# Two stages changed at once: 7x7 filter rows loaded to half of the partitions and copied across by VectorE, and a last pass whose first layer runs in three parts of two slices instead of two parts of three

## The chip, the cores and the metric

One NeuronCore of a Trainium2 chip runs the whole program. The metric is device time in microseconds (us): the median of several executions. All arithmetic is float32. The engines are named as in the profile: PE is TensorE (matmuls), PEld is its weight load, DVE is VectorE, ACT is ScalarE, POOL is GpSimd, SP is SyncE, which here only issues transfers. Transfers can be issued from SP, ACT or POOL.

## The reference, cut to what matters

The input `x` is 8 images of 96 x 96 pixels with 192 channels. Two residual blocks follow one another. The first has a projection to 384 channels, a 3x3 depthwise convolution, four directional scans, a layer norm and a projection back. The second, which is the one that the change touches, is

```python
def _L1_conv_ref(x, dw_kernel, dw_bias, ln_gamma, ln_beta, w0, b0, w1, b1, gamma):
    y = lax.conv_general_dilated(x, dw_kernel, window_strides=(1, 1), padding='SAME',
            dimension_numbers=('NHWC', 'HWIO', 'NHWC'), feature_group_count=c) + dw_bias   # 7x7 depthwise
    mu = jnp.mean(y, axis=-1, keepdims=True)
    var = jnp.mean(jnp.square(y - mu), axis=-1, keepdims=True)
    y = (y - mu) * lax.rsqrt(var + EPS) * ln_gamma + ln_beta
    y = jnp.einsum('bhwc,cd->bhwd', y, w0) + b0        # first layer: 192 -> 768
    y = jax.nn.gelu(y, approximate=False)
    y = jnp.einsum('bhwd,dc->bhwc', y, w1) + b1        # second layer: 768 -> 192
    return y * gamma

x = x + _L0_conv_ref(_gn(x), ...)
x = x + _L1_conv_ref(_gn(x), ...)                      # _gn: group norm with 32 groups of 6 channels
```

## The kernel before

The program has five stages, one after another. A projects to 384 channels, B convolves 3x3 and scans, C normalizes and projects back, D makes the 7x7 convolution, E is the last pass: layer norm, first layer, Gelu, second layer. Only D and E are touched.

**Stage D.** The convolution is a product with banded matrices. There are 32 steps `m` of `HC` = 6 channels each. A step needs the image rows `xin` and the filter's band `band`, both as tiles of 128 partitions. Partitions 0 to 63 and 64 to 127 hold two different blocks of image rows, and the band is the same in both halves, so it is loaded twice from DRAM:

```python
    def load_d(m):
        c = m * HC
        ...
        pool = d_pools[m % ND > 0]                       # ND = 5 tiles of each kind in all
        xin = pool.tile([128, NT, BP, HC, 2 * WV], F32, tag="xin", name="xin")
        for t in range(NT):                              # NT = 3
            for g, eng in enumerate((nc.sync, nc.gpsimd)):
                ...
                eng.dma_start(xin[g * 64 : (g + 1) * 64, t].rearrange(...), src)
        band = pool.tile([128, HC, ZW], F32, tag="band", name="band1")   # ZW = 208
        for g, eng in enumerate((nc.sync, nc.gpsimd)):
            eng.dma_start(
                band[g * 64 : (g + 1) * 64].rearrange("q c l -> q (c l)"),
                Z2_d[:, c : c + HC].rearrange("r c l -> r (c l)"),
            )
        return band, xin
```

`scale_d` applies the group norm to a loaded `xin` in eight VectorE instructions; the convolution of a pair of steps follows, and its result is stored to DRAM from POOL:

```python
        def scale_d(m, xin):
            xv = xin.rearrange("q t a c (v b) -> q t a c v b", b=2)
            for b in range(B):                           # B = 8
                ...
                nc.vector.tensor_scalar(xw, xw, sc, sh, ALU.mult, ALU.add)

            loads = [first_d] + [load_d(m) for m in range(1, 3)]
            ...
            for i in range(n_i):                         # n_i = 16 pairs
                pair, loads = loads[:2], loads[2:]
                for m in (2 * i + 3, 2 * i + 4):
                    if m < 2 * n_i:
                        loads.append(load_d(m))
                if i + 1 < n_i:
                    for k in range(2):
                        scale_d(2 * i + 2 + k, loads[k][1])
                yo = op.tile([128, NB, BP * NV, HC, 2 * WQ], F32, tag="yo", name=f"yo_{i}")
                for c in range(HC):
                    conv_d(pair, c, yo, i)               # 432 PE instructions for each pair
                store_d(yo, i)
```

The convolution's matmul is line L1021, the store's issues are L1060 (SP) and L1061 (POOL), the loads' issues are L748 (`xin`) and L753 (`band`), the scaling is L1006.

**Stage E.** There are `n_u` = 96 units of 4 x 96 x 2 pixels. Each unit is transposed (`turn_in`, three calls), taken through the first layer into `g` with Gelu on ACT, and through the second layer (`second_layer`, three calls). The 192 input channels of the first layer are 128 + 64: the 128 go as a full matmul, the 64 as a matmul on half of the array's rows, where those of the two images (`q`) lie in different halves:

```python
        ps_t = ph.enter_context(tc.tile_pool(name="e_ps_t", bufs=1, space=PSUM))
        ps_h = ph.enter_context(tc.tile_pool(name="e_ps_h", bufs=7, space=PSUM))
        ...
        def first_layer(u, mb):
            ...
            ms = range(mb * NE // 2, (mb + 1) * NE // 2)     # NE = 6: three slices of 128 of the 768
            for m in ms:
                for q in range(2):
                    hps[m, q] = ps_h.tile([128, WH * S], F32, tag="hp", name="hp")
                    nc.tensor.matmul(hps[m, q], w0w[:, 2 * q, ...], yT[:, 2 * q], start=True, stop=False)   # L1183
            for m in ms:
                for q in range(2):
                    p = slice(q * DH, (q + 1) * DH)          # DH = 64
                    nc.tensor.matmul(hps[m, q], w0w[p, 1, ...], yT[p, 1], start=False, stop=True)           # L1193
            for m in ms:
                for q in range(2):
                    nc.scalar.activation(g[:, m, q], hps[m, q], AF.Gelu, ...)                               # L1202

        def second_layer(u, k):
            ...
            po = ps_h.tile([128, 2, D], F32, tag="hp", name="po")
            for q in range(2):
                for m in range(NE):
                    nc.tensor.matmul(po[:, q], g[:, m, q, k * 128 : (k + 1) * 128], w1g[:, m], ...)         # L1213
            nc.vector.tensor_tensor(xo[:, k]..., po..., rs_[u][:, k], ALU.add)
            ...
```

The order of the calls for a unit (conditions on the first and last units cut):

```python
            for u in range(n_u + 1):
                first_layer(u, 0)
                turn_in(u + 1, 0); load_r(u + 1)
                bias_r(u)
                stats_e(u + 2, j)              # j = 0..3
                second_layer(u - 1, 0)
                turn_in(u + 1, 1)
                first_layer(u, 1)
                turn_in(u + 1, 2)
                stats_e(u + 2, j)              # j = 4..7
                second_layer(u - 1, 1)
                norm_e(u + 2, j)               # j = 0..7
                second_layer(u - 1, 2)
```

Of the kernel before, what the change touches and what calls it, by code (L numbers as in the profile page):

```python
# [8 lines left out]
F32 = mybir.dt.float32  # L9
# [3 lines left out]
PSUM = bass.MemoryType.PSUM  # L13
# [71 lines left out]
def conv_blocks_kernel(  # L85
# [31 lines left out]
    nc = tc.nc  # L117
# [617 lines left out]
    def load_d(m):  # L735
        c = m * HC
        row = D * WV * 2
        pool = d_pools[m % ND > 0]
        xin = pool.tile([128, NT, BP, HC, 2 * WV], F32, tag="xin", name="xin")

        for t in range(NT):
            for g, eng in enumerate((nc.sync, nc.gpsimd)):
                src = bass.AP(
                    tensor=X1_d.tensor,
                    offset=X1_d.offset + (2 * t + g) * HG * PH * row + c * WV * 2,
                    ap=[[row, 64], [S * PH * row, BP], [1, HC * WV * 2]],
                )
                eng.dma_start(  # L748
                    xin[g * 64 : (g + 1) * 64, t].rearrange("q a c n -> q a (c n)"), src
                )  # L750
        band = pool.tile([128, HC, ZW], F32, tag="band", name="band1")
        for g, eng in enumerate((nc.sync, nc.gpsimd)):
            eng.dma_start(  # L753
                band[g * 64 : (g + 1) * 64].rearrange("q c l -> q (c l)"),
                Z2_d[:, c : c + HC].rearrange("r c l -> r (c l)"),
            )
        return band, xin

    s1 = s1_pool.enter_context(tc.tile_pool(name="s1", bufs=1)).tile(
# [228 lines left out]
    with ExitStack() as ph:  # L988
        cp = ph.enter_context(tc.tile_pool(name="d_const", bufs=1))
        d_pools[1] = ph.enter_context(tc.tile_pool(name="d_in", bufs=ND - 1))  # L990
        op = ph.enter_context(tc.tile_pool(name="d_out", bufs=2))
        ps_y = ph.enter_context(tc.tile_pool(name="d_ps", bufs=4, space=PSUM))

        dwb = cp.tile([128, D // CD, HC], F32, name="dwb")
        for k in range(2):
            nc.scalar.dma_start(
                dwb[k * 64 : (k + 1) * 64],
                dw_bias.rearrange("(i k c) -> k i c", k=2, c=HC)[k].partition_broadcast(64),
            )

        def scale_d(m, xin):
            xv = xin.rearrange("q t a c (v b) -> q t a c v b", b=2)
            for b in range(B):
                sc, sh = (s1[:, a, b % 2, b // 2, m : m + 1] for a in range(2))
                xw = xv[:, :, b // 2, :, :, b % 2]
                nc.vector.tensor_scalar(xw, xw, sc, sh, ALU.mult, ALU.add)  # L1006

        def conv_d(pair, c, yo, i):

            pys = [  # L1010
                [ps_y.tile([128, 2, BP, 2 * WV], F32, tag=f"py{a}", name=f"py{a}")
                 for _ in range(2)]
                for a in range(2)
            ]
            for t in range(NT):
                for n, d in enumerate((1, 0, 2)):
                    lo, hi = 2 * max(0, 1 - d), 2 * (WV - max(0, d - 1))
                    for k in range(2):
                        for g in range(2):
                            rows = slice(g * 64, g * 64 + KB)  # L1020
                            nc.tensor.matmul(  # L1021
                                pys[t // 2][g][k * 64 : (k + 1) * 64, t % 2, :, lo:hi],
                                pair[k][0][rows, c, d * ZS : d * ZS + 64],
                                pair[k][1][rows, t, :, c, lo + 2 * (d - 1) : hi + 2 * (d - 1)],
                                start=(n == 0),
                                stop=(n == 2),
                            )
                if t == 0:
                    continue
                for g in range(2):  # L1030
                    bl = slice(g, 4 + g, 2) if t == 1 else slice(4 + g, 5 + g)
                    nc.scalar.activation(
                        yo[:, bl, :, c],
                        pys[t // 2][g][:, : 2 - t // 2].rearrange("q t b (a v) -> q t (b a) v", a=NV),
                        AF.Identity,
                        bias=dwb[:, i, c : c + 1],
                        scale=1.0,
                    )

        def store_d(yo, i):  # L1040
            for bl in range(NB):

                pieces = [(3, HB - 3)]
                if bl == 0:
                    pieces.append((HB - 3, HB))
                if bl == NB - 1:
                    pieces.append((0, 3))
                for k in range(2):
                    c = i * CD + k * HC
                    for lo, hi in pieces:  # L1050
                        r = (S - HB - bl * HG) * PH
                        src = yo[k * 64 + lo * PH : k * 64 + hi * PH, bl]
                        dst = Y_d[r + lo * PH : r + hi * PH, :, :, c : c + HC].rearrange(
                            "r b a c n -> r (b a) (c n)"
                        )
                        src = src.rearrange("r a c n -> r a (c n)")

                        n = NV if i == D // CD - 1 else 0
                        if n:
                            nc.sync.dma_start(dst[:, :n], src[:, :n])  # L1060
                        nc.gpsimd.dma_start(dst[:, n:], src[:, n:])  # L1061

        n_i = D // CD
        with tc.manual_schedule():
            loads = [first_d] + [load_d(m) for m in range(1, 3)]
            make_weights(ps_y.tile([128, 512], F32, tag="py1", name="ps_b0"))
            for m in range(2):
                scale_d(m, loads[m][1])
            for i in range(n_i):
                pair, loads = loads[:2], loads[2:]  # L1070
                for m in (2 * i + 3, 2 * i + 4):
                    if m < 2 * n_i:
                        loads.append(load_d(m))
                if i + 1 < n_i:
                    for k in range(2):
                        scale_d(2 * i + 2 + k, loads[k][1])
                yo = op.tile([128, NB, BP * NV, HC, 2 * WQ], F32, tag="yo", name=f"yo_{i}")
                for c in range(HC):
                    conv_d(pair, c, yo, i)
                store_d(yo, i)  # L1080
    s1_pool.close()

# [8 lines left out]
    with ExitStack() as ph:  # L1094
        ip = ph.enter_context(tc.tile_pool(name="e_in", bufs=2))
        sp = ph.enter_context(tc.tile_pool(name="e_small", bufs=3))
        tp = ph.enter_context(tc.tile_pool(name="e_t", bufs=2))
        ps_t = ph.enter_context(tc.tile_pool(name="e_ps_t", bufs=1, space=PSUM))
        ps_h = ph.enter_context(tc.tile_pool(name="e_ps_h", bufs=7, space=PSUM))

        def place(n):
            bp, n = divmod(n, PH * NV)
# [25 lines left out]
        def bias_r(u):  # L1128
            r = rs_[u].rearrange("p k (b c) -> p (k b) c", b=2)
            nc.gpsimd.tensor_tensor(  # L1130
                r, r, b1g.unsqueeze(1).to_broadcast([128, 2 * S // HE, D]), ALU.add
            )
# [41 lines left out]
        def first_layer(u, mb):  # L1174
            if mb == 0:
                gs[u] = tp.tile([128, NE, 2, WH * S], F32, tag="g", name="g")
            yT, g = yTs[u].rearrange("p k h j -> p k (h j)"), gs[u]
            ms = range(mb * NE // 2, (mb + 1) * NE // 2)
            hps = {}
            for m in ms:  # L1180
                for q in range(2):
# [24 lines left out]
        def second_layer(u, k):  # L1206
            if k == 0:
                xos[u] = tp.tile([128, S // HE, 2, D], F32, tag="xo", name="xo")
            g, xo = gs[u], xos[u]
            po = ps_h.tile([128, 2, D], F32, tag="hp", name="po")  # L1210
            for q in range(2):
                for m in range(NE):
                    nc.tensor.matmul(  # L1213
# [22 lines left out]
        with tc.manual_schedule():  # L1236
# [8 lines left out]
                    for k in range(3):  # L1245
                        turn_in(0, k)
            for u in range(n_u + 1):

                if u < n_u:
                    first_layer(u, 0)  # L1250
                if u + 1 < n_u:
                    turn_in(u + 1, 0)
                    load_r(u + 1)
                if u < n_u:
                    bias_r(u)
                if u + 2 < n_u:
                    for j in range(4):
                        stats_e(u + 2, j)
                if u >= 1:
                    second_layer(u - 1, 0)  # L1260
                if u + 1 < n_u:
                    turn_in(u + 1, 1)
                if u < n_u:
                    first_layer(u, 1)
                if u + 1 < n_u:
                    turn_in(u + 1, 2)
                if u + 2 < n_u:
                    for j in range(4, WE):
                        stats_e(u + 2, j)
                if u >= 1:  # L1270
                    second_layer(u - 1, 1)
                if u + 2 < n_u:
                    for j in range(WE):
                        norm_e(u + 2, j)
                if u >= 1:
                    second_layer(u - 1, 2)


# [45 lines left out]
```

## Time and profile before

The time before is 6060.05 us, the median of three executions from 6058.6 to 6065.66 us. The profiled execution has a span of 6063.8 us.

| stretch of the span | what runs | PE busy | granted PE clock | DMA share | GB/s |
|---|---|---|---|---|---|
| 2900 to 3012 us | end of C | 101.98 of 112 us | 0.98 | 0.78 | 233 |
| 3012 to 3062 us | C to D | 9.52 of 50 us | 0.50 | 0.90 | 238 |
| 3062 to 3540 us | D | 366.98 of 478 us | 0.86 | 1.05 | 284 |
| 3540 to 3631 us | D to E | 44.62 of 91 us | 0.74 | 0.74 | 182 |
| 3631 to 3700 us | E fills | 62.01 of 69 us | 0.92 | 0.25 | 66 |
| 3700 to 6040 us | E | 2340.00 of 2340 us | 1.00 | 0.25 | 69 |

The table comes from the view that gives each engine's busy time by stretch. "DMA share" is the mean busy share of the core's 16 DMA engines; it sums the times of packets, so that overlapping packets can bring it slightly over 1. Over the whole span PE is busy for 5662.7 us (93%), DVE for 3455.4 us (57%), POOL for 2650.1 us (44%) and ACT for 2427.9 us (40%). A matmul of this float32 program shows as two PE instructions, so twelve calls in the code are 24 in the profile. The durations of single matmuls overlap in the record; the distance from one start to the next is what a matmul costs.

### The profile page before, as it was taken

The page shows a single profiled execution, that of the slowest core. Times are in us where ns is not written, and L with a number is a line of the kernel's source. Part 1 is how long each engine was busy: PE and PEld are TensorE (multiplying, and loading weights), DVE is VectorE, ACT ScalarE, POOL GpSimd, SP SyncE. Part 2 cuts the span into 40 slices and gives each one's busy share as a digit, 9 for nine tenths or more (in the row PEclk, how much of TensorE's full clock was granted, in tenths as well). Part 3 has the DMA queues.
Part 4 walks back from the last instruction along what each step waited for, and adds up shares of the span by engine and source line. Part 5 has one row for each costly group of instructions (what it writes and reads, how often), then busy time and mean ns, then how long its engine had stood idle before and what let it go on. Part 6 is the DMA issues. An engine that isn't in the chain of part 4 may idle for free.

```text
span 6063.8 us, 122727 instructions
## 1 busy us (share of the span) xinstructions
PE 5662.7 (93%) x48550; PEld 3970.7 (65%) x48550; DVE 3455.4 (57%) x8026; ACT 2427.9 (40%) x6146; POOL 2650.1 (44%) x2832
## 2 busy tenths in 40 slices
PE   4799989999998999999867759999999999999999
PEld 2455543333334989898756647777777777777777
DVE  5455539999996667777723225444444444444443
ACT  1344437777775555555433322222222222222221
POOL 0111118888886666666534433333333333333332
PEclk9999989999999999999988879999999999999999
DMA  8977759999997888888799982222222222222221
GB/s 235 230 242 226 231 175 243 243 243 244 245 246 203 248 263 264 263 267 262 233 275 284 291 211 60 74 70 72 74 68 76 67 79 63 79 63 79 63 63 38
DMA packets 570206, 1054.36 MB, mean 174 GB/s; under 512 B 109575, under 2 KB 426260, under 8 KB 567328
## 3 DMA queue, kind: packets, MB, share of 16 engines
q1 hardware_dynamic: 385312, 577.65, 36.1%
q0 software_dynamic: 124160, 450.67, 24.1%
q10 hardware_dynamic: 60160, 18.20, 1.5%
q8 instruction: 384, 6.29, 0.5%
q14 instruction: 190, 1.56, 0.1%
HBM read 585.19 MB, written 476.57 MB: 175 GB/s over the span
## 4 chain that ended last, share of the span: by engine, by line
PE 76%; DMA 6%; DVE 1%; issue 1%; SPq 1%; POOL 1%; ACT 0%; DVEq 0%; POOLq 0%; ACTq 0%
PE po L1213 19%; PE po L830 13%; PE hp L1183 12%; PE pl L576 10%; PE hp L1193 7%; PE pa L597 4%; PE pt L828 4%; DMA xin<-X_d 4%; PE py L1021 3%; PE pa L600 2%; PE pt L1166 2%; DMA Y_d<-yo 1%; DVE xin L1006 1%; DMA band<-Z_d 0%; SPq L1060 0%
## 5 line engine op out<-in xcount | busy, mean ns | idle before, releaser
L1202 ACT ACTIVATE g<-hp,b0g 128x384 f32<-128x384 f32 x1152 | 563.5, 587 | 1831.5 <-PE hp L1193 1831.4
L1213 PE MATMUL po<-w1g,g 128*128 128x192 f32 x6912 | 1160.0, 327 | 0.0
L1213 PEld LDWEIGHTS po<-w1g,g 128*128 128x128 f32 x6912 | 1118.8, 190 | 1.1 <-issue 1.1
L830 PE MATMUL po<-wc,mt 128*96 128x193 f32 x4608 | 913.1, 334 | 0.0
L1170 DVE COPY yT<-pt 128x384 f32<-128x384 f32 x288 | 250.0, 868 | 1044.7 <-PE pt L1166 1044.4
L1183 PE MATMUL hp<-yT,w0w 128*128 128x384 f32 x2304 | 781.4, 489 | 0.4 <-DVE yT L1170 0.4
L830 PEld LDWEIGHTS po<-wc,mt 128*96 128x96 f32 x4608 | 702.0, 163 | 68.4 <-ACT mean L834 65.0
L1231 POOL DMA_DIRECT2D out_dram<-xo x576 | 340.2, 593 | 880.9 <-DVE xo L1220 853.7
L576 PE MATMUL pl<-pin,band 34*32 34x380 f32 (+1 forms) x13824 | 628.2, 489 | 18.5 <-DMA pin<-P_d 18.5
L1183 PEld LDWEIGHTS hp<-yT,w0w 128*128 128x128 f32 x2304 | 429.4, 191 | 257.3 <-issue 3.3
L1021 PE MATMUL py<-xin,band 63*64 63x248 f32 (+1 forms) x6912 | 409.0, 396 | 140.7 <-DVE xin L1006 134.9
L606 DVE TENSOR_TENSOR_SCAN z<-decay,loc 128x768 f32<-128x768 f32 x288 | 505.9, 1756 | 58.5 <-ACT loc L585 28.5
L646 POOL TENSOR_TENSOR mo<-mo,z 128x768 f32<-128x768 f32 x288 | 528.9, 1837 | 3.3 <-ACT mo L601 0.2
L29 POOL TENSOR_TENSOR rs<-rs_ve,neg_half 96x8 f32<-96x8 f32 x96 | 158.6, 1652 | 826.3 <-DVE rs_ve L28 826.3
L615 DVE TENSOR_TENSOR_SCAN z<-decay,z 128x768 f32<-128x768 f32 x288 | 498.2, 1730 | 0.0
L576 PEld LDWEIGHTS pl<-pin,band 34*32 34x32 f32 x13824 | 232.0, 107 | 396.6 <-issue 394.5
L1021 PEld LDWEIGHTS py<-xin,band 63*64 63x64 f32 x6912 | 344.4, 143 | 204.9 <-DVE xin L1006 121.2
L837 ACT ACTIVATE sq<-pt,mean 96x384 f32<-96x384 f32 x768 | 442.9, 577 | 25.9 <-ACT mean L834 1.0
L597 PE MATMUL pa<-loc,mix 128*32 128x384 f32 x3456 | 431.7, 493 | 0.0
L375 PE MATMUL pm<-xT,win 128*128 128x384 f32 x1152 | 408.3, 506 | 21.6 <-ACT xT L368 21.1
L600 PE MATMUL pa<-last,down 96*32 96x384 f32 x1152 | 426.6, 493 | 0.9 <-ACT mo L601 0.9
L1193 PE MATMUL hp<-yT,w0w 64*128 64x384 f32 x2304 | 423.5, 500 | 0.0
(116 smaller groups left out, 7726.4 us busy)
## 6 DMA issues: line engine op xcount, KB each, us to landing
P_d<-po POOLq DMA_DIRECT2D x96, 1152.0 KB, 8.8
pin<-P_d SPq DMA_DIRECT2D x192, 576.0 KB
mt<-M_d SPq DMA_DIRECT2D x576, 192.0 KB
xq<-in_x_dram SPq DMA_DIRECT2D x96, 576.0 KB
xr<-in_x_dram SPq DMA_DIRECT2D x384, 144.0 KB
X_d<-x1u POOLq DMA_DIRECT2D x192, 288.0 KB, 4.2
X_d<-x1c SPq DMA_DIRECT2D x192, 288.0 KB
y<-Y_d SPq DMA_DIRECT2D x24, 2304.0 KB
```

Source lines behind the costliest of these rows:

```text
L576: nc.tensor.matmul(pls[g][at * RB : (at + 1) * RB, :, lo:hi], band[rows, c, kh, :], pin[rows, c, :, NJ - 1 - j, lo + kh - 1 : hi + kh - 1] ...
L597: nc.tensor.matmul(pa[at], mix[:, i, at], loc[:, q], start=True, stop=True)
L600: nc.tensor.matmul(pa[at], down[:, to], last[:, q], start=True, stop=True)
L606: nc.vector.tensor_tensor_scan(zf, decay_f, loc.rearrange("p q n -> p (q n)"), 0.0, ALU.mult, ALU.add)
L615: nc.vector.tensor_tensor_scan(zr, decay_f, zr, 0.0, ALU.mult, ALU.add)
L646: nc.gpsimd.tensor_tensor(m, m, z, ALU.add)
L830: nc.tensor.matmul(po[:S, b], lhs[m], wc[:, m], start=(m == 0), stop=(m == NC - 1))
L1021: nc.tensor.matmul(pys[t // 2][g][k * 64 : (k + 1) * 64, t % 2, :, lo:hi], pair[k][0][rows, c, d * ZS : d * ZS + 64], pair[k][1][rows, t, ...
L1183: nc.tensor.matmul(hps[m, q], w0w[:, 2 * q, m * 128 : (m + 1) * 128], yT[:, 2 * q], start=True, stop=False,)
L1193: nc.tensor.matmul(hps[m, q], w0w[p, 1, m * 128 : (m + 1) * 128], yT[p, 1], start=False, stop=True,)
L1202: nc.scalar.activation(g[:, m, q], hps[m, q], AF.Gelu, bias=b0g[:, m : m + 1], scale=1.0)
L1213: nc.tensor.matmul(po[:, q], g[:, m, q, k * 128 : (k + 1) * 128], w1g[:, m], start=(m == 0), stop=(m == NE - 1),)
```

## The change

The change has two parts that have nothing to do with each other.

In D, step `m` loads the band to one half of the partitions only: for even `m` to the lower half from SP, for odd `m` to the upper half from POOL. VectorE then copies it to the other half, ahead of the eight scaling instructions of the same step. It is meant to take bytes from the DMA engines.

In E, the first layer is cut into three parts of two slices (four PSUM banks for a part) instead of two parts of three (six banks). The eight PSUM banks are given out anew: two for the transposes, four for the first layer, and two of its own for the second layer. Each of the three thirds of a unit is then alike: a part of the first layer, a transpose, a part of the second layer.

```diff
         band = pool.tile([128, HC, ZW], F32, tag="band", name="band1")
-        for g, eng in enumerate((nc.sync, nc.gpsimd)):
-            eng.dma_start(
-                band[g * 64 : (g + 1) * 64].rearrange("q c l -> q (c l)"),
-                Z2_d[:, c : c + HC].rearrange("r c l -> r (c l)"),
-            )
+
+        g = m % 2
+        (nc.sync, nc.gpsimd)[g].dma_start(
+            band[g * 64 : (g + 1) * 64].rearrange("q c l -> q (c l)"),
+            Z2_d[:, c : c + HC].rearrange("r c l -> r (c l)"),
+        )
         return band, xin
...
-        def scale_d(m, xin):
+        def scale_d(m, band, xin):
+            g = m % 2
+            nc.vector.tensor_copy(
+                band[(1 - g) * 64 : (2 - g) * 64], band[g * 64 : (g + 1) * 64]
+            )
             xv = xin.rearrange("q t a c (v b) -> q t a c v b", b=2)
...
-        ps_t = ph.enter_context(tc.tile_pool(name="e_ps_t", bufs=1, space=PSUM))
-        ps_h = ph.enter_context(tc.tile_pool(name="e_ps_h", bufs=7, space=PSUM))
+        ps_t = ph.enter_context(tc.tile_pool(name="e_ps_t", bufs=2, space=PSUM))
+        ps_h = ph.enter_context(tc.tile_pool(name="e_ps_h", bufs=4, space=PSUM))
+        ps_o = ph.enter_context(tc.tile_pool(name="e_ps_o", bufs=2, space=PSUM))
...
-            ms = range(mb * NE // 2, (mb + 1) * NE // 2)
+            ms = (2 * mb, 2 * mb + 1)
...
-            po = ps_h.tile([128, 2, D], F32, tag="hp", name="po")
+            po = ps_o.tile([128, 2, D], F32, tag="po", name="po")
...
             for u in range(n_u + 1):
-                ... (the order of calls shown above)
+                for k in range(3):
+                    if u < n_u:
+                        first_layer(u, k)
+                    if u + 1 < n_u:
+                        turn_in(u + 1, k)
+                    if k == 0:
+                        if u + 1 < n_u:
+                            load_r(u + 1)
+                        if u < n_u:
+                            bias_r(u)
+                    if u + 2 < n_u:
+                        if k < 2:
+                            for j in range(4 * k, 4 * k + 4):
+                                stats_e(u + 2, j)
+                        else:
+                            for j in range(WE):
+                                norm_e(u + 2, j)
+                    if u >= 1:
+                        second_layer(u - 1, k)
```

More of the change, by code (lines that the diff above doesn't have):

```diff
@@ L1067, in conv_blocks_kernel @@
             for m in range(2):
-                scale_d(m, loads[m][1])
+                scale_d(m, *loads[m])
             for i in range(n_i):
@@ L1075, in conv_blocks_kernel @@
                     for k in range(2):
-                        scale_d(2 * i + 2 + k, loads[k][1])
+                        scale_d(2 * i + 2 + k, *loads[k])
                 yo = op.tile([128, NB, BP * NV, HC, 2 * WQ], F32, tag="yo", name=f"yo_{i}")
@@ L1247, in conv_blocks_kernel @@
             for u in range(n_u + 1):
[L1249 to L1276, printed above, removed]
+                for k in range(3):
[17 more added lines that the diff above has]
+                        second_layer(u - 1, k)
 _INS = [
```

## The prediction

> **What bounds the kernel now.** The change touches D and E only, so I read the profile by stage. First, busy time by stretch. D in steps of 20 us (columns: stretch, length, busy us of PE, PEld, DVE, ACT, POOL with counts, PE clock, DMA share, GB/s):
>
> ```profile
> 3200.00:3220.00 20.00, 20.00 (x369) 17.26 (x364) 4.01 (x7) 10.47 (x20) 10.67 (x17) 0.96 1.03 314
> 3220.00:3240.00 20.00, 13.14 (x220) 10.84 (x216) 9.53 (x16) 6.26 (x12) 9.62 (x15) 0.83 1.05 269
> 3240.00:3260.00 20.00, 13.64 (x260) 11.42 (x252) 1.99 (x4) 8.41 (x16) 8.38 (x14) 0.90 1.05 279
> 3260.00:3280.00 20.00, 17.19 (x292) 14.93 (x296) 7.66 (x13) 7.54 (x15) 10.38 (x16) 0.84 1.05 340
> 3280.00:3300.00 20.00, 10.72 (x178) 8.81 (x172) 4.81 (x9) 5.03 (x10) 6.37 (x11) 0.76 1.05 240
> ```
>
> PE pauses, DVE is idle most of the time, and the DMA share never leaves 1.03 to 1.05: the DMA engines have no room anywhere. Next, the waits between 3000 and 3600 us (who waited for what: us in total, times, longest):
>
> ```profile
> DVE xin L1006 <- DMA xin<-X_d: 370.3, 31, 26.3
> ...
> PE py L1021 <- DVE xin L1006: 134.9, 17, 20.6
> ```
>
> DVE waits for loaded rows, PE waits for DVE's scaling: 17 waits, one for each pair. The starts of the convolutions in the trace are 33.3 us apart (3196.66 to 3530.01 us is ten pairs), of which PE works 25 and waits 8. D is bound by transfers.
>
> E is the opposite: PE is busy for 2340.00 of 2340 us at clock 1.00, and DMA is at 0.25. The chain that ended last, in order of time, shows one unit (start, length, instruction, count):
>
> ```profile
> 4000.99 7.83 PE po L1213 x48
> 4008.81 3.87 PE hp L1183 x12
> 4012.68 2.14 PE hp L1193 x12
> 4014.82 0.48 PE pt L1166 x4
> 4015.30 3.93 PE po L1213 x24
> 4019.23 0.33 PE pt L1166 x4
> 4019.56 3.90 PE hp L1183 x12
> 4023.46 2.14 PE hp L1193 x12
> 4025.60 0.48 PE pt L1166 x4
> 4026.08 7.83 PE po L1213 x48
> ```
>
> A unit takes 25.09 us, and nothing but PE is on the chain. So E's time is the number of matmuls and the joints between unlike ones. The same transposes take 0.48 us behind a half-array group (L1193) but 0.33 us behind the second layer (L1213). The weight load shows the joint too (waits from 3700 to 6000 us):
>
> ```profile
> PEld hp L1193 <- issue: 99.7, 183, 0.5
> PEld pt L1166 <- issue: 99.7, 183, 0.5
> ```
>
> Each of 183 changes into and out of a half-array group makes the weight load stand 0.54 us with nothing to wait for; the matmuls behind it lose less, since they run on meanwhile.
>
> **What the Trainium skill says.** "TensorEngine Tiling (Array Packing)", Key Properties: a change of the tiling mode drains TensorE. The trace agrees: full matmuls of the first layer start 322.5 ns apart, but the first half-array one starts 416 ns after the last full one, the second pair 420 ns after the first where later pairs take 322, and the first transpose 413 ns after the last pair. "VectorE: DVE Perf Modes", perf-mode tier table: a float32 copy from SBUF to SBUF runs at two elements a cycle. A contiguous float32 scaling of 768 elements (L718) takes 615 ns here, under the 800 ns that one a cycle of its 0.96 GHz would need, so the trace fits. "DMA: Bandwidth & Descriptors", Issuing engines are not separate DMA queues: transfers of SP and POOL share the same 16 engines. D's share of 1.05 whether one or both queues move agrees. "SBUF — State Buffer", two separate sides: such a copy keeps GpSimd from writing the descriptors of its own transfers; no copy of this kind runs beside POOL's transfers before, so nothing here shows what it costs.
>
> **Part one, D: what it removes.** One band load is 64 partitions x 1248 x 4 B = 319,488 B; 32 of the 64 go, 10.2 MB. In the trace, the packets of the loads that disappear (SP's for odd steps, POOL's for even ones) took 17.9 + 20.2 = 38.1 us when summed and divided by 16 engines. With a share of 1.05 that is 36 us of DMA time, or 2.3 us a pair: the upper end. Not all of it need come back. Counting packets in stretches of 2 us, POOL's queue moves only 200 GB/s while it loads alone (380 ns for a packet of 4608 B), but the two queues together 300 to 400. Each pair has some 23.5 us with both and 9.8 us with POOL alone. If SP keeps its own pace, 11% fewer bytes on SP shorten the first stretch to 21 us, in which POOL moves less. Of POOL's 6.54 MB, now 6.22, about 4.09 then pass in the first stretch and 2.13 MB are left, 10.65 us at 200 GB/s: 31.65 us a pair, a gain of 1.65. That is the lower end: 16 x 1.65 = 26 us. I take the middle, **31 us**.
>
> What it adds: 32 copies of 64 x 1248. From L718's 615 ns for 768 elements, between 0.8 us (adding half a cycle for each further element) and 1.0 us (in proportion). DVE is busy for 28 of 100 us in D and has room for two a pair. The copy also makes the scaling wait for the band, which lands after the rows. So rows to convolution grows by some 2.5 us (319,488 B behind the rows at 200 GB/s are 1.6, the copy 0.9). In the steady state that is free, because PE's pause of 8 us takes it: a convolution of 25 us started 2.5 us later still ends before POOL's queue reaches its stores. At the first pair it is not hidden: +2 us.
>
> **Part two, E.** No instruction goes or comes; the groups are cut differently. A third of the new unit is 8 full, 8 half-array, 4 transposes, 24 of the second layer. From the lines above:
> - 8 full: 3.87 less four at 0.3225 = 2.58 us
> - 8 half-array: 2.14 less two pairs at 0.3225 = 1.50 us
> - transposes behind a half-array group: 0.48 us
> - second layer: 3.93 us
>
> Sum 8.49, times three 25.46 us, against 25.09: **+0.36 us for a unit, 35 us for 96**. It is the third half-array group with its two changes of mode. Nothing hides it, PE being the chain. The new bank split should add no wait: Gelu of four banks takes about 4 x 0.49 = 2 us (six take 2.93 in the trace), and the next part needs them 4.4 us after its group ends (0.48 + 3.93). At the start of E two transpose banks save two waits of 0.93 us, and the first unit's shorter part meets the norm of the next unit earlier and waits some 2 us longer: zero.
>
> **Sum:** 6060 - 31 + 2 + 35 = 6066; the two sizes point against each other, and I shade to **6065 us**.
>
> **Rivals.**
> 1. *The band was hidden anyway, or the delay takes its place.* If D is bound by the loop of buffer free, load, scale, convolve rather than by bytes, the copy and the later band lengthen the loop, and D gains nothing or loses 10 us. For it: SP waits for PE to free buffers (261.1 us, 14 times). Against: POOL's queue always has work and the share never falls below 1.02 in the steady state. Time then 6095 to 6105.
> 2. *The copies hold up POOL's descriptors.* 32 us of copies, if all were lost to the queue that bounds D, would undo the gain: 6095. Against: POOL issues well ahead of its transfers (12.8 us from issue to landing), so a pause of 1 us should not empty the queue.
> 3. *The three-part order saves waits in E.* Separate banks could do so if banks were the limit. Against: PE has no idle time from 3700 to 6040 us. If the joints cost nothing after all, 6031.
> 4. *D gains more,* because fewer bytes let PE's clock rise from 0.86: PE is not D's bound, so no.
>
> **Range and chances.** D's gain of 26 to 36, E's loss of 33 to 36 and 3 us of spread between executions give 6057 to 6073 if nothing else happens. For a part of rivals 1 and 2, and for an underrated relief of D, I widen to 6050 to 6084. Two per cent is 121 us, and no rival reaches it.
>
> **What would show it.** In the profile after: D's pairs 31.0 to 31.7 us apart with a DMA share still at 1.05; DVE copies `band<-band` of 0.8 to 1.0 us; E's unit 25.45 us in the chain, with three half-array groups of about 1.5 us each and the weight load's 0.54 us before 6 groups a unit instead of 4. Wrong if D's pairs stay at 33 us or the share falls below 1 (rivals 1, 2), or if E's unit stays at 25.1 us (rival 3), or if ACT's Gelu comes onto the chain.

## The result: 0.5% slower, and the profile after

The changed kernel takes 6091.97 us (median of four, 6082.58 to 6095.32) against 6059.33 us before: a ratio of 1.0049, 95% interval 1.0032 to 1.0067, or some 30 us more. The prediction was 6065 us with a range of 6050 to 6084, so the result lies outside. E lost what was predicted. D did not give what was predicted.

E first. The chain that ended last in the changed kernel, in order of time (start, length, instruction, count), shows one unit (from D's scaling on, line numbers are 5 higher than before: L1188 was L1183, L1198 was L1193, L1026 was L1021):

```profile
4000.14 2.58 PE hp L1188 x8
4002.72 1.49 PE hp L1198 x8
4004.22 0.48 PE pt L1171 x4
4004.70 3.93 PE po L1218 x24
4008.62 2.58 PE hp L1188 x8
4011.20 1.49 PE hp L1198 x8
4012.70 0.48 PE pt L1171 x4
4013.18 3.93 PE po L1218 x24
4017.11 2.58 PE hp L1188 x8
4019.68 1.49 PE hp L1198 x8
4021.18 0.48 PE pt L1171 x4
4021.66 3.93 PE po L1218 x24
4025.59 2.58 PE hp L1188 x8
```

The next unit starts at 4025.59, so a unit takes 25.45 us where it took 25.09. Each line is within 0.01 us of the length that the prediction worked out for it. From E's first full matmul to the end of the program are 2433.2 us before (from 3630.65 us) and 2465.5 us after (from 3626.27 us), 32.3 us more.

D now, by busy time in steps of 20 us (columns as in the prediction):

```profile
3200.00:3220.00 20.00, 18.96 (x360) 16.06 (x352) 0.00 (x0) 11.26 (x22) 7.02 (x13) 1.00 1.02 257
3220.00:3240.00 20.00, 13.96 (x212) 11.84 (x216) 11.46 (x18) 5.00 (x10) 11.53 (x18) 0.74 1.03 317
3240.00:3260.00 20.00, 14.16 (x249) 11.99 (x244) 7.24 (x12) 7.73 (x15) 8.72 (x15) 0.97 0.99 224
3260.00:3280.00 20.00, 17.36 (x276) 12.88 (x272) 4.10 (x7) 7.38 (x14) 8.17 (x14) 0.85 1.05 277
3280.00:3300.00 20.00, 13.86 (x205) 9.87 (x200) 11.36 (x18) 5.73 (x12) 8.48 (x13) 0.83 0.97 248
```

The share dips to 0.97 and the rates are lower: over the ten pairs from the fourth to the fourteenth, 269 GB/s after against 288 before. Those ten pairs took 335.9 us after and 334.5 before; 6 MB less went through in nearly the same time. (From the fifth to the fifteenth it is 330.2 against 333.4 us, so a difference of a few us over ten pairs says nothing.) In these two traces the last convolution of D ended 2.4 us earlier (3581.2 against 3583.6 us), and that is all that came of the band's bytes. The waits between 3000 and 3600 us say where to look:

```profile
DVE band L1004 <- DMA band<-Z_d: 271.2, 14, 27.0
...
POOL Y_d L1066 <- ACT yo L1037: 145.5, 19, 27.0
PE py L1026 <- DVE xin L1011: 125.6, 16, 19.3
```

and of SP's queue:

```profile
SPq L748 <- PE py L1026: 294.0, 15, 33.1
```

VectorE now waits for the band where it waited for the rows. POOL waits 145.5 us for a convolution's results before it can store them, against 92.5 us before, and SP waits 294.0 us for a convolution to free its tiles, against 261.1. POOL's queue, which I had taken for never empty, runs out at the seams between pairs. At one of them:

```profile
3288.00:3290.00 2.00, 0.25 (x8) 0.00 (x0) 1.61 (x3) 1.09 (x3) 2.00 (x4) 1.00 0.56 107
```

The DMA share is 0.56 there.

### The profile page after: what moved, and what is told of

The parts are those of the page before. It is cut to its first block, busy times and chain, and to the rows that moved or that the text cites. A ratio compares the mean times of both kernels' runs of the same rounds, so it can differ in the third digit from the quotient of the medians.

```text
span 6091.8 us, 122792 instructions
## 1 busy us (share of the span) xinstructions
PE 5697.4 (94%) x48550; PEld 3942.0 (65%) x48550; DVE 3484.5 (57%) x8058; ACT 2438.8 (40%) x6146; POOL 2623.2 (43%) x2816
## 4 chain that ended last, share of the span: by engine, by line
PE 77%; DMA 6%; DVE 1%; SPq 1%; issue 1%; POOL 0%; ACT 0%; POOLq 0%; ACTq 0%; DVEq 0%
PE po L1218 19%; PE po L831 13%; PE hp L1188 12%; PE pl L576 10%; PE hp L1198 7%; PE pa L597 4%; PE pt L829 4%; PE py L1026 3%; DMA xin<-X_d 3%; PE pt L1171 2%; PE pa L600 2%; DMA Y_d<-yo 2%; DVE xin L1011 1%; DMA band<-Z_d 0%; SPq L1065 0%
## 5 line engine op out<-in xcount | busy, mean ns | idle before, releaser
L1218 PE MATMUL po<-w1g,g 128*128 128x192 f32 x6912 | 1178.3, 327 | 0.0
L1236 POOL DMA_DIRECT2D out_dram<-xo x576 | 321.3, 560 | 1148.1 <-DVE xo L1225 1119.6
L1188 PE MATMUL hp<-yT,w0w 128*128 128x384 f32 x2304 | 795.5, 489 | 0.4 <-ACT g L1207 0.4
L1188 PEld LDWEIGHTS hp<-yT,w0w 128*128 128x128 f32 x2304 | 431.8, 191 | 232.0 <-issue 3.2
L606 DVE TENSOR_TENSOR_SCAN z<-decay,loc 128x768 f32<-128x768 f32 x288 | 505.9, 1756 | 59.4 <-ACT loc L585 29.6
L1026 PE MATMUL py<-xin,band 63*64 63x248 f32 (+1 forms) x6912 | 408.8, 394 | 138.1 <-DVE xin L1011 125.6
L1026 PEld LDWEIGHTS py<-xin,band 63*64 63x64 f32 x6912 | 335.2, 142 | 211.3 <-DVE xin L1011 112.7
L1198 PE MATMUL hp<-yT,w0w 64*128 64x384 f32 x2304 | 449.6, 509 | 0.0
```

The costliest lines, as they stand in the source:

```text
L606: nc.vector.tensor_tensor_scan(zf, decay_f, loc.rearrange("p q n -> p (q n)"), 0.0, ALU.mult, ALU.add)
L1026: nc.tensor.matmul(pys[t // 2][g][k * 64 : (k + 1) * 64, t % 2, :, lo:hi], pair[k][0][rows, c, d * ZS : d * ZS + 64], pair[k][1][rows, t, ...
L1188: nc.tensor.matmul(hps[m, q], w0w[:, 2 * q, m * 128 : (m + 1) * 128], yT[:, 2 * q], start=True, stop=False,)
L1198: nc.tensor.matmul(hps[m, q], w0w[p, 1, m * 128 : (m + 1) * 128], yT[p, 1], start=False, stop=True,)
```

## The experiments

All experiments start from the kernel before and change D, except `e_only`. Each comparison is with the kernel before on the same chip. The last column is the ratio less one, times the median before. The ratios of `all_sp` and `rows_sp` leave out one slow execution each, of 11,781 and 28,453 us.

| run | what differs from before | median, us | before, us | ratio, 95% interval | us |
|---|---|---|---|---|---|
| `d_only` | D as changed | 6062.06 | 6058.73 | 1.0010 (1.0002 to 1.0017) | +6 |
| `e_only` | E as changed | 6087.45 | 6058.73 | 1.0046 (1.0034 to 1.0058) | +28 |
| `copy_only` | both loads, and the copy | 6075.34 | 6058.73 | 1.0031 (1.0020 to 1.0043) | +19 |
| `no_copy` | half load, no copy, no wait | 6040.21 | 6058.73 | 0.9971 (0.9960 to 0.9982) | -18 |
| `band_first` | D as changed, band ahead of the rows | 6055.74 | 6057.51 | 0.9996 (0.9988 to 1.0003) | -2 |
| `copy_late` | D as changed, copy behind the scaling | 6053.59 | 6057.51 | 0.9991 (0.9983 to 0.9999) | -5 |
| `all_sp` | D as changed, every band from SP | 6056.99 | 6057.51 | 0.9993 (0.9985 to 1.0002) | -4 |
| `rows_sp` | both loads, a third of POOL's rows from SP | 6069.26 | 6057.51 | 1.0017 (1.0010 to 1.0024) | +10 |
| `dummy_copy` | both loads, copies that wait for nothing | 6056.06 | 6059.14 | 0.9998 (0.9988 to 1.0008) | -1 |
| `wait_only` | half load, the wait, no copy | 6059.00 | 6059.14 | 0.9999 (0.9991 to 1.0007) | -1 |
| `copy_act` | half load, copy by ScalarE | 6045.62 | 6059.14 | 0.9978 (0.9970 to 0.9986) | -13 |
| `odd_sp` | both loads, odd steps from SP, even from POOL | 6060.09 | 6060.65 | 1.0006 (0.9997 to 1.0016) | +4 |
| `odd_sp_act` | `copy_act` in that order | 6024.56 | 6060.65 | 0.9950 (0.9933 to 0.9967) | -30 |
| `odd_sp_dve` | D as changed in that order | 6031.69 | 6057.43 | 0.9954 (0.9941 to 0.9968) | -28 |

**First question: which half of the change, and is it bytes or the chain?** Theory 1: the saved bytes are real, but the chain load, wait, copy, scale, convolve, store grew by as much. Theory 2, the rival: the bytes were hidden all along. `d_only` and `e_only` each take one half of the change's diff. `copy_only` keeps the double load and adds the copy:

```diff
-        def scale_d(m, xin):
+        def scale_d(m, band, xin):
+            g = m % 2
+            nc.vector.tensor_copy(band[(1 - g) * 64 : (2 - g) * 64], band[g * 64 : (g + 1) * 64])
```

`no_copy` loads like the change without copying. The other half of each tile keeps the filter of five steps ago, so part of the filter is left out; convolution and transfers are the change's:

```diff
+        if m < ND:
+            bands[m] = pool.tile([128, HC, ZW], F32, tag=f"band{m}", name=f"band{m}", bufs=1)
+        band = bands[m % ND]
         for g, eng in enumerate((nc.sync, nc.gpsimd)):
-            eng.dma_start(band[g * 64 : (g + 1) * 64]..., Z2_d[:, c : c + HC]...)
+            if m < ND or g == m % 2:
+                eng.dma_start(band[g * 64 : (g + 1) * 64]..., Z2_d[:, c : c + HC]...)
```

Expected of `d_only`:

> Only the band's half load and copy; E as before. Both theories: 6055 to 6059 us, that is 0 to 5 us less than before, since the convolution ended only 2.4 us earlier in the changed kernel's profile. If it is 20 us or more less than before, the loss arises from the two parts together and both theories fall.

Expected of `e_only`:

> Only the three-part last pass; D as before. Both theories: +32 us (6092), from 0.36 us for each of 96 units less about 2 us at the start of E. If it is below +25 us, the joints are not what E lost.

Expected of `copy_only`:

> Both band loads stay, and VectorE copies one half over the other ahead of the scaling: the copy and the wait for the band without any bytes saved. Theory 1 (the longer chain load, copy, scale, convolve, store eats what the bytes save): slower than before by 15 to 35 us, about 1 to 2.5 us for each of 16 pairs. Theory 2 (the band's bytes were hidden anyway and the copy costs nothing): within 4 us of before.

Expected of `no_copy`:

> The transfers of the change without its copy: five lasting bands, both halves loaded for the first five steps only, then one half by turns; the other half keeps the filter of five steps ago (this leaves out part of the filter, so the numbers computed are others; instructions and times of the convolution stay the same). Theory 1: faster than before by 20 to 33 us (D's pairs 31.2 to 31.8 us apart). Theory 2: within 5 us of before, pairs still 33 us apart.

Measured: +6, +28, +19 and -18 us. `d_only` came out a little slower than both theories allowed, `no_copy` 2 us short of theory 1's window. The loss is nearly all E's, the two halves add up (6 + 28 = 34 against a measured 30, whose interval is 19 to 41), and theory 2 falls: without wait and copy the bytes are worth 18 us, with them they are gone. In the trace of `no_copy` the pairs are 31.8 us apart on average (33.1 before).

**Second question: the wait, or the copy itself?** A third theory was that VectorE's copy costs by itself, because it keeps GpSimd from writing descriptors (the prediction's rival 2). `band_first` moves the band's load ahead of the rows in `load_d`. `copy_late` copies behind the eight scaling instructions. `all_sp` and `rows_sp` move work between the queues:

```diff
 # all_sp
-        g = m % 2
-        (nc.sync, nc.gpsimd)[g].dma_start(
+        g = 0
+        nc.sync.dma_start(
 # rows_sp
-            for g, eng in enumerate((nc.sync, nc.gpsimd)):
+            for g, eng in enumerate((nc.sync, nc.gpsimd if t < 2 else nc.sync)):
```

Expected of `band_first`:

> D with the half load and the copy, E as before, but the band is loaded ahead of the rows of its step in place of behind them, so that the copy can run while the rows still arrive. Same bytes and same copies as in the run with D alone. Theory 1 (the wait for the band and the copy lengthen the chain): nearly all of the run without copies comes back, 12 to 20 us less than before (6039 to 6047). Theory 3 (the copy costs by itself, because it keeps GpSimd from writing its descriptors): stays within 5 us of before, like the run with D alone.

Expected of `copy_late`:

> D with the half load, E as before; VectorE copies the band behind the eight scaling instructions, not ahead of them. The scaling no longer waits for the band, only the 0.8 us of the copy are added to the chain. Theory 1: the wait for the band is the larger part, so 6 to 14 us less than before (6045 to 6053). If it is the same as the run with D alone, the wait for the band costs nothing and the copy itself is the cost (theory 3).

Expected of `all_sp`:

> D with the half load and the copy, E as before; every half load comes from SP, none from POOL. POOL's queue, which is the longer one, loses two loads a pair in place of one, and the band of an odd step lands with SP's rows, some 8 us ahead of POOL's. Theory 1: at least as fast as the run without copies, 18 to 35 us less than before. Theory 3: within 5 us of before.

Expected of `rows_sp`:

> D and E as before with both band loads, but the third of the three row loads of the upper half comes from SP in place of POOL. No byte and no copy more or less: it moves 1 MB a pair from POOL's queue, which also carries the stores and loads alone at 200 GB/s for 10 of 33 us, to SP's. If POOL's queue is D's limit rather than the bytes, faster by 20 to 60 us; if the sum of the bytes is the limit, within 8 us of before.

Measured: -2, -5, -4 and +10 us. Theory 1 as I had put it missed `band_first` and `all_sp`, and `copy_late` fell 1 us short of its window of 6 to 14. `rows_sp` missed both of its expectations: POOL's queue is not D's limit by its length, since `rows_sp` made it shorter and D slower, and with the same bytes it did not stay within 8 us either. Theory 3 fitted `band_first` and `all_sp`. So I tried the copy and the wait each alone:

```diff
 # dummy_copy: in scale_d, both band loads kept
+            for _ in range(2):
+                nc.vector.tensor_copy(spare[(1 - g) * 64 : (2 - g) * 64], spare[g * 64 : (g + 1) * 64])
 # wait_only: in scale_d, on top of no_copy
+            nc.vector.tensor_copy(spare[h, m : m + 1], band[h, 0, 0:1])
 # copy_act: in place of VectorE's copy; called behind conv_d of the pair before
+            nc.scalar.copy(band[(1 - g) * 64 : (2 - g) * 64], band[g * 64 : (g + 1) * 64])
```

Expected of `dummy_copy`:

> Everything as before (both band loads), plus VectorE copies of a tile of its own ahead of each step's scaling: two of 64x576 a step, about 0.45 us each, which wait for no load. They fall into VectorE's idle time. Theory 3 (a copy of this kind holds up GpSimd and with it POOL's transfers): 10 to 20 us slower than before. Theory 1 (only the chain through wait and copy counts): within 4 us of before.

Expected of `wait_only`:

> Like the run without copies (lasting bands, half loads after the fifth step, part of the filter thus left out), but ahead of each step's scaling VectorE copies one element a partition of the newly loaded half into a tile of its own, so the scaling waits for the band as in the change. Theory 1: the wait (about 1.6 us a pair behind the rows) costs 8 to 25 us of the 18 us that the run without copies gained, so 6048 to 6065. Theory 3: stays at the run without copies, 6038 to 6046.

Expected of `copy_act`:

> D with the half load, E as before; the copy is ScalarE's, placed behind the evacuation of the pair before, beside VectorE's scaling. VectorE's scaling no longer waits for the band, and no VectorE copy runs. Theory 1 and theory 3 both: 10 to 20 us less than before (6038 to 6048). If it is within 4 us of before, the copy costs wherever it runs, and both fall short.

Measured: -1, -1 and -13 us. Theory 3 falls: as many microseconds of VectorE copies that wait for nothing (64 of 0.46 us) cost nothing, though 44 of POOL's 365 issues overlapped one. An instruction of one element a partition that waits for the band takes back the 18 us of `no_copy` (intervals -24 to -11 us there, -5 to +4 us here). Its trace, waits between 3000 and 3600 us:

```profile
DVE spare L1008 <- DMA band<-Z_d: 350.6, 17, 29.5
```

and busy time by stretch for `no_copy`,

```profile
3200.00:3500.00 300.00, 237.53 (x4016) 198.93 (x4012) 87.27 (x144) 116.32 (x223) 135.66 (x211) 0.87 1.02 275
```

then for `wait_only`:

```profile
3200.00:3500.00 300.00, 221.54 (x3799) 189.65 (x3790) 82.85 (x152) 111.11 (x212) 125.58 (x199) 0.86 1.00 262
```

The same transfers at the same share within 2%, but 5% fewer bytes a second and 5% fewer matmuls: the wait leaves the DMA engines with less to do at the seams.

**Third question: why did loading the band earlier not help?** Theory 4, which was formed after the results above, counts the bytes that have to pass, after a pair's convolution has ended, until the odd step that the next but one pair waits for is complete: the stores (3.54 MB), SP's rows of two steps (2.36) and POOL's rows of one (1.18), and every band load that comes on SP or that the scaling waits for on POOL (0.32 each). Before, that is 3.54 + 2.36 + 1.18 + two bands on SP = 7.72 MB, POOL's own band being hidden behind the scaling. `d_only`, `wait_only` and `band_first` have one band on SP and now wait for POOL's: 7.72. `all_sp` has two on SP and none on POOL: 7.72. Only `no_copy`, `copy_late` and `copy_act` come to 7.40. The difference of 0.32 MB at the 275 GB/s of `no_copy` is 1.16 us, for 16 pairs 18.6 us: what `no_copy` gained. `rows_sp` adds 0.4 MB and `copy_only` 0.32 MB and a copy, and both were slower. To test it I changed the order and nothing else: from step 3 on, all loads of odd steps from SP, where no store stands ahead of them, and those of even steps from POOL.

```diff
 # odd_sp, in load_d
+        queues = (nc.sync, nc.gpsimd) if m < 3 else ((nc.gpsimd, nc.sync)[m % 2],) * 2
-            for g, eng in enumerate((nc.sync, nc.gpsimd)):        # rows and band
+            for g, eng in enumerate(queues):
```

Expected of `odd_sp`:

> D and E as before with both band loads and no copy; but from step 3 on all loads of an odd step come from SP and all loads of an even step from POOL. Same bytes, the same split between the two queues. Theory 4 (what counts is how many bytes the engines must move, after a pair's convolution ends, until the next but one pair's odd step is complete: stores 3.54 MB, SP's rows of two steps, POOL's rows of one): the odd step no longer stands behind the stores, so 20 to 45 us less than before (6014 to 6039). If only the sum of the bytes, or the length of POOL's queue, decides: within 8 us of before.

Expected of `odd_sp_act`:

> As odd_sp, with the band's half load (odd steps from SP, even ones from POOL) and the copy by ScalarE behind the evacuation. Theory 4 with the bytes saved on top: 5 to 30 us less than odd_sp. If the bytes of the band are hidden once the order is right, within 5 us of odd_sp.

Measured: +4 us, a clear miss for theory 4 alone, and -30 us, that is 36 less than `odd_sp`, more than the 5 to 30 expected. The order is worth nothing while the band is loaded twice, and it doubles the gain (-13 to -30) once it is loaded once. That led to theory 5: a pair takes the longer of two times that lay within a microsecond of each other, the bytes through the DMA engines and the loop. Its test is the changed D itself, with VectorE's copy and its wait, in the new order:

Expected of `odd_sp_dve`:

> The change's D exactly (half load, VectorE's copy ahead of the scaling, the wait for the band), E as before, only with the loads of odd steps from SP and those of even steps from POOL. Theory 5 (a pair takes the longer of two: the bytes through the DMA engines, 33 us with the band twice and 31 with it once, and the loop of convolution, stores, loads, wait and copy, also 33 us in the old order): the new order shortens the loop, so the wait and the copy fit beside the transfers and the saved bytes show: 20 to 40 us less than before (6020 to 6040). If the copy or the wait on VectorE costs in itself, it stays within 8 us of before while the same order with ScalarE's copy gave 36 us.

Measured: -28 us (19 to 36). Busy time over ten whole pairs, from the fourth convolution to the fourteenth, of `odd_sp`,

```profile
3151.12:3476.60 325.48, 258.48 (x4320) 206.82 (x4320) 96.68 (x160) 125.55 (x240) 144.26 (x228) 0.88 1.03 286
```

and of `odd_sp_dve`:

```profile
3166.57:3462.78 296.21, 247.95 (x4321) 221.50 (x4321) 112.80 (x180) 126.08 (x240) 150.75 (x232) 0.91 1.04 305
```

and its wait for the band between 3000 and 3600 us:

```profile
DVE band L1004 <- DMA band<-Z_d: 276.2, 27, 25.8
```

VectorE waits for the band as long as in the changed kernel (271.2 us there), yet the DMA engines stay at 1.04 and move 305 GB/s. In this order the wait costs nothing that shows: -28 us with it, -30 us without it in `odd_sp_act`. That the loop has slack here is theory 5's reading; no run measured the slack. Nor does theory 5 say why the rate rose from 286 to 305 GB/s at about the same share. The pairs of this run are 30.7 us apart on average. With E left as before, the versions `odd_sp_dve` and `odd_sp_act` beat both kernels.

## Why the prediction was wrong

**E: right.** The sum of 2.58, 1.50, 0.48 and 3.93 us for a third of a unit came out at 2.58, 1.49, 0.48 and 3.93. The predicted +35 us stand against +32.3 us in the trace and +28 us (21 to 35) in `e_only`. The units give 96 x 0.36 = 35 us; the 2 us between lie within the scatter of E's length from trace to trace (2430.7 to 2436.0 us with E as before). The weight load's unexplained pause ahead of half-array groups (waits from 3700 to 6000 us) is there three times a unit:

```profile
PEld hp L1198 <- issue: 147.7, 271, 0.5
```

That is 271 where there were 183: three groups a unit in place of two. The new banks added no wait on the chain, as predicted.

**D: the bytes were there to be gained, but not in the order of the change.** `odd_sp_act` and `odd_sp_dve` gained 30 and 28 us, inside the prediction's 26 to 36 us. That is no proof of the working from packets. Over the ten pairs above, a pair of `odd_sp_dve` took 29.6 us against 32.5 in `odd_sp`, 2.9 us less where the packets gave at most 2.3, and the rate was higher (305 against 286 GB/s); so part of its gain may be the rate and not the bytes. In the order of the change the saved bytes brought nothing: +6 us in `d_only`.

**The step that failed** is this one: "In the steady state that is free, because PE's pause of 8 us takes it: a convolution of 25 us started 2.5 us later still ends before POOL's queue reaches its stores." The pause of 8 us was not slack. By the order of the code and the waits shown above, it was the visible part of a loop as long as the period: SP's loads start when a convolution frees the tiles, POOL's loads stand behind the stores of that convolution, and the next but one convolution waits for both. Fewer bytes shortened the one limit, and the wait held the other where it was. `wait_only` measures the wait alone: it takes the whole 18 us that `no_copy` gained. The loop itself is argued; what speaks for it is that another order of the same loads made the same wait and copy harmless.

**What I misread** was the share of 1.05. I took it as proof that the sum of the bytes was the only limit. It tells that the engines have a packet in hand, not how fast it goes: in nearly the same share POOL's loads alone moved 200 GB/s and loads beside stores 300 to 400. Two stretches of the kernel before show it:

```profile
3216.00:3218.00 2.00, 2.00 (x44) 1.75 (x40) 0.00 (x0) 0.98 (x2) 1.26 (x3) 1.00 1.02 197
3242.00:3244.00 2.00, 2.00 (x46) 1.74 (x40) 0.00 (x0) 1.03 (x3) 0.46 (x1) 1.00 1.06 389
```

A later start of SP's loads shows as a lower rate first and as a lower share (1.00 to 1.02) only second.

**The rivals.** Rival 1, that the later band takes the place of what the bytes give, was the right one, and its 6095 us was close; I had put it aside on the ground of the share. Its other half, that the bytes were hidden anyway, is refuted by `no_copy`. Rival 2 is refuted by `dummy_copy`, and by `odd_sp_dve`, which has the change's own copies and gains 28 us. The copies were predicted at 0.8 to 1.0 us and took 0.83 us on average; by the prediction's own rule (0.615 us and half a cycle for each of 480 further elements) the lower end is 0.87, so that they were a little cheaper than it had worked out. Its narrow range is mis-summed as well, by little: its terms give 6054 to 6073 us, not 6057 to 6073.

**What stays open.** The count of 7.72 and 7.40 MB was argued from the order of the queues. It failed in `odd_sp`, and in the old order it does not fit each size: `copy_only` should by it have lost 1.16 + 0.8 us a pair, 31 us, and lost 19; `d_only`, `band_first` and `all_sp` should each have lost the copy's 0.8 us a pair, 13 us, and came out at +6, -2 and -4. Theory 5 rests on one run foretold, `odd_sp_dve`. A rival was not tested: the new order may gain because more of the loads pass beside stores. SP's row packets took 93 ns on average over the ten pairs of `odd_sp` and 80 ns in `odd_sp_dve`. How the two limits share a pair where they are nearly equal was not measured further.

## What to carry to other kernels

A stage that looks bound by transfers can at the same time be held by a loop of about the same length: buffer free, load, work, store. Then a wait added to the loop can take back what fewer bytes give, as it did here. Before counting bytes as time, write down what must have landed ahead of the step that the next wait ends on, queue by queue, and see whether the change makes that smaller. Cutting the same matmuls into more groups was not free where full and half-array matmuls meet: one more half-array group cost 0.36 us in each of 96 units here.

## What the runs showed of the hardware

- A DMA share of 1.02 to 1.08 went with 200 to 400 GB/s (stretches of 2 us in the kernel before). By the order of the issues, POOL's load packets of 4608 B took 380 ns while they ran alone, and its store packets of the same size 190 ns. SP's row packets of 1536 B took 68 ns beside those stores. With loads from both queues at once, in `odd_sp`, SP's took about 120 ns and POOL's about 320 ns, and 220 to 260 GB/s went through.
- VectorE copies of 64x1248 float32 took 0.80 us. POOL's transfer issues that overlapped them took longer (0.81 against 0.65 us on average in `d_only`, 29 of 350); longer issues are also likelier to overlap. Copies of 64x576 cost no time in D (`dummy_copy`).
- Moving a third of POOL's row loads to SP made D slower by 10 us, though POOL's queue was the longer one.
- In the kernel before, POOL's issues waited mostly for the transfer issued exactly eight earlier on POOL: 139 of the 156 waits over 0.15 us that a transfer ended from 3080 to 3500 us. So a store can also wait for rows to land (80.2 us in all between 3000 and 3600 us).
